# Four row-tiled products in a visit, one ring of five PSUM banks, three products per tile into one accumulator bank

## The chip, the cores and the metric

The kernel runs on one core of one Trainium2 chip. The metric is the device time in microseconds (us) of one launch, from three runs. The engines are named as in the profile: PE (TensorE matmuls), PEld (its weight loads), DVE (VectorE), ACT (ScalarE), POOL (GpSimd), SP (SyncE, which issues most DMAs).

## The reference, cut to what matters

The reference is a layer of a perceiver: cross-attention of 512 latent rows over 8192 context rows, then a Mamba-like block with an MLP, then a mixture of 16 experts with a shared expert. The change touches the cross-attention, and the tail through the PSUM banks that it hands on.

```python
x = x + xattn(layernorm(x), ctx, ctx, Wq, bq, Wk, bk, Wv, bv, Wo, bo)   # x 512x512, ctx 8192x512
x = x + attn(layernorm(x), ...)      # state-space block, MLP
x = x + ffn(layernorm(x), ...)       # 16 experts, top 2, shared expert

def xattn(Q, K, V, ...):             # 16 heads of 64
    q = (1 / 8) * (Q @ Wq + bq);  k = K @ Wk + bk;  v = V @ Wv + bv
    a = softmax(einsum('nlhd,nshd->nhls', q, k))
    o = einsum('nhls,nshd->nlhd', a, v)
    return o @ Wo + bo
```

## The kernel before

**Precision by splitting.** The kernel is held to float32 accuracy with float16 products. An operand is split into a high and a low float16 part, and a product is made of three: high x high, high x low, low x high.

**Passes.** The 16 heads are 8 pairs, and a pass (`filler`, L421) works for two pairs at a time, so there are 4 passes (`NPASS`). Each goes over the context in 16 chunks of 512 rows (`NCH`). For a chunk it makes the keys of both pairs (`kproj_units`, L246, two groups of 12 products of 512 columns), and the values (`vproj_units`, L266, two groups of 24 products of 256 columns), and stores them in DRAM (`k_d`, `v_d`). A value row of a head holds low part (64), a zero, high part (64) and a constant 16: `VW` = 130.

**Maximum pass.** Softmax needs each row's maximum before the exponentials. `smax_units` (L286) makes a rough score of the chunk for it, from the high parts alone. The contraction is 64 long, so the two heads of a pair stand in the upper and the lower 64 rows of PE, and their two products (L297, 512 columns) can run side by side. ACT copies each bank to `sf` (L302), and DVE takes the running maximum (L310) once four copies are there. One turn of this is called a visit here. In the first pass (`wide`) a visit has four products, in two pairs, with banks of `ps_x` and `ps_s`; in passes 2 to 4 it has two, with the two banks of `ps_x`, and `yield 406` after each.

**Attention.** A unit is a pair of heads and half of the 512 rows (16 units), and has 32 steps of 256 context rows (`NSTEP`). `scores` (L345) makes 8 products of 256 columns (L359, L360) into two banks of `ps_s`, 2 to a bank and head; ACT takes the exponential to float32 (L367, two instructions). In even steps ACT takes it a second time to float16 for the high part (L369); in odd steps DVE casts it (L371). DVE subtracts for the low part (L372). `av` (L375) multiplies with the values: 8 products of 130 columns with the high part as weights (L389), which give high x low and high x (high, row sum) side by side, and 8 of 65 columns with the low part (L392). They pile up over the 32 steps in `po0` and `po1`, a bank for each head. `unit_end` (L394) adds the halves, divides by the row sum, turns the result (L410, a bank of `bank_j`) and splits it.

**PSUM.** There are 8 banks: `ps_s` 2, `ps_o` 2 (`po0`, `po1`), `ps_x` 2, `ps_j` 2. `bank_j` (L126) hands out banks for projections and turns; outside of the attention it also uses `po1`. The tail's accumulators (`acc`, L647) use `ps_s`, `po0` and `ps_x`.

**Order.** The order of PE is written by hand up to the last unit (`manual_schedule`); the order of the other engines, and of PE after that, is a scheduler's. The filler is a generator that yields the planned PE time of each piece: 648 ns for 3 products of 512 or 6 of 256 columns, 406 for a visit of two. After every second piece (fourth in the first pass) `pump` gives one visit. The first pass runs alone. Passes 2 to 4 are woven into the first 380 steps (`NFILL`, L560): a step is scores, then pieces worth half of `rate`, then the `av` of an earlier step, then pieces worth the other half (L575 to L591). `rate` is the planned time of three passes (`PASSN`) over 380. The steps after that have no filler, and take the banks of `ps_x` for the scores of odd steps. The 16th unit is woven with the start of the tail (`tail`, L630), which does the rest of the layer. `weight_prep` (L509) brings in and splits the tail's weights on DVE in the first 380 steps, block by block as they land.

Of the kernel before, what the change touches and what calls it, by code (L numbers as in the profile page):

```python
# [16 lines left out]
P = 128  # L17
# [11 lines left out]
VW = 130  # L29
# [4 lines left out]
PASSN = 16 * (4 * 2592 + 8 * 406) + 2 * 2592 + 600  # L34
# [3 lines left out]
def perceiver_layer(ctx: ExitStack, tc: tile.TileContext, a: dict, out: bass.AP):  # L38
# [83 lines left out]
    ps_x = ctx.enter_context(tc.tile_pool(name="ps_x", bufs=2, space=PSUM))  # L122
    ps_j = ctx.enter_context(tc.tile_pool(name="ps_j", bufs=2, space=PSUM))
    jn = [0, True]

    def bank_j(shape, dtype, name):  # L126

        if jn[1]:
            jn[0] += 1
            if jn[0] % 3 == 0:  # L130
                return ps_o.tile(shape, dtype, name=name, tag="po1")
        return ps_j.tile(shape, dtype, name=name, tag="pj")
# [22 lines left out]
    for t in vss:  # L155
        nc.gpsimd.memset(t[:, :, :, 64:65], 0.0)
        nc.gpsimd.memset(t[:, :, :, 129:130], WS)
# [108 lines left out]
    def vproj_units(g, c, ct, w, j):  # L266
# [13 lines left out]
        nc.scalar.copy(vs[:, :, :, 65:129], pv)  # L280
        nc.vector.tensor_tensor(vs[:, :, :, 0:64], pv, vs[:, :, :, 65:129], ALU.subtract)  # L281
# [4 lines left out]
    def smax_units(c, qh, kh, runm, wide):  # L286

        for q2 in range(2):
            sf = sb3.tile([P, 2, 2, CH], F16, name="sf", bufs=2)
            pss = []  # L290
            for qi in range(2):
                qt = 2 * q2 + qi
                for hh in range(2):
                    s = slice(hh * 64, hh * 64 + 64)
                    pool, tag = (ps_s, "pss") if wide and qi else (ps_x, "px")
                    ps = pool.tile([P, CH], F32, name="psx", tag=tag)
                    nc.tensor.matmul(ps, lhsT=qh[s, qt * P : (qt + 1) * P], rhs=kh[s, 0, :], start=True, stop=True)  # L297
                    pss.append((sf[:, qi, hh, :], ps))
                if wide and not qi:
                    continue  # L300
                for dst, ps in pss:
                    nc.scalar.activation(dst, ps, AF.Copy, scale=1.0 / (8.0 * WS))  # L302
                pss = []
                if not qi:
                    yield 406
# [5 lines left out]
            yield 626 if wide else 406  # L311
# [33 lines left out]
    def scores(u, m, ld, sp, alone=False):  # L345
# [6 lines left out]
        for i in range(2):  # L352
            t = (m % 4) * 2 + i
            sl = slice(t * P, (t + 1) * P)
            pool, tag = (ps_x, "px") if alone and m % 2 else (ps_s, "pss")
            ps = pool.tile([P, 2, HQ], F32, name="pss", tag=tag)
# [18 lines left out]
    def av(po, m, x):  # L375
# [3 lines left out]
        for x in range(2):  # L379
            for i in range(2):  # L380
                t = (m % 4) * 2 + i
                for hh in range(2):
                    vv = v[:, t, hh]
                    for qt in range(2):
                        o, qs = po[hh][:, qt, :], slice(qt * P, (qt + 1) * P)
                        first = m == 0 and i == 0 and qt == 0
                        last = m == NSTEP - 1 and i == 1
                        if x == 0:
                            nc.tensor.matmul(o, lhsT=ph[:, i, hh, qs], rhs=vv, start=first, stop=False, **kw)  # L389
                        else:  # L390
                            o, vv_ = o[:, 65:VW], vv[:, 65:VW]
                            nc.tensor.matmul(o, lhsT=pl[:, i, hh, qs], rhs=vv_, start=False, stop=last, **kw)  # L392

    def unit_end(u, po, sp):  # L394
# [26 lines left out]
    def filler():  # L421
# [23 lines left out]
        for g in range(NPASS):  # L445
# [14 lines left out]
            for c in range(NCH):  # L460
# [93 lines left out]
    jn[1] = False  # L554
# [10 lines left out]
    def drain():  # L565
        pu, pm, px = pend.pop(0)
        if pm == 0:
            po[:] = [ps_o.tile([P, 2, VW], F32, name=f"po{hh}", tag=f"po{hh}") for hh in range(2)]
        av(po, pm, px)
        if pm == NSTEP - 1:  # L570
            e = unit_end(pu, po, sp[0])
# [33 lines left out]
    for m in range(NSTEP):  # L605
# [7 lines left out]
        if m == 0:  # L613
            tl = tail(tc, a, out, const, scr, ident, x_sb, mlp_d, oT, y_d, xd_d, (ps_s, ps_o, ps_x, bank_j))
# [7 lines left out]
    jn[1] = True  # L622
# [7 lines left out]
def tail(tc, a, out, const, scr, ident, x_sb, mlp_d, oT, y_d, xd_d, psums):  # L630
# [5 lines left out]
    ps_s, ps_o, ps_x, bank_j = psums  # L636
# [722 lines left out]
```

## Time and profile before

| what | us |
|---|---|
| median of 3 runs (lowest, highest) | 2652.26 (2648.97, 2652.97) |
| profiled execution | 2653.45 |
| its span, first to last instruction | 2651.7 |
| first pass alone | 0 to 278.5 |
| steps 1 to 380, with passes 2 to 4 | 278.5 to 1644.6 |
| steps 381 to 480 | 1644.6 to 1809.8 |
| last unit, with the start of the tail | 1809.8 to 1914.5 |
| tail | 1914.5 to 2651.7 |

The stretches are cut at the starts of the score products. The granted PE clock over the span is 0.959 of full speed.

The costliest groups that the change touches; columns: line, engine, operation, out<-in, shape, count, busy us, mean ns of one, idle time of the engine before them and who ended it:

```profile
L302 ACT ACTIVATE sf<-psx 128x512 f16<-128x512 f32 x1024 | 557.7, 622 | 79.1 <-PE psx L297 77.2
L389 PE MATMUL po<-v,phl 128*128 128x130 f16 x4096 | 327.2, 222 | 5.2 <-DVE oq L402 4.7
L297 PE MATMUL psx<-khl,qh 64*128 64x512 f16 x1024 | 212.5, 395 | 21.3 <-ACT sf L302 18.4
L392 PE MATMUL po<-v,phl 128*128 128x65 f16 x4096 | 209.9, 194 | 9.3 <-DVE phl L372 9.3
```

The mean length of a matmul is the time from its start to its end, and matmuls overlap: a product of 65 columns is 194 ns long, while eight of them follow each other within 0.24 us. So what a product costs PE is read from the distance of two starts, in the view that lists instructions in order of time. The busy time of a group counts overlapping instructions once.

### The profile page before, as it was taken

To read this page: it belongs to the slowest core of one execution; us is meant where nothing else is said; L and a number is where in the kernel's file an instruction comes from. 1 tells how busy PE (TensorE), PEld (TensorE's weight loads), DVE (VectorE), ACT (ScalarE), POOL (GpSimd) and SP (SyncE) were. 2 spreads that over 40 slices of the span, in tenths; PEclk is the share of its full clock that TensorE was granted. 3 is DMA by queue.
4 is the path that set the end of the run, shared out by engine and by line. 5 is a ranking of instruction groups with operands and counts; after the bars stand their busy time and mean duration, and the time that the engine had idled before them with its cause. 6 is when DMAs were issued, how large, how long until landed. Compare 5 with 4: busy or idle time off the path is not lost. (4 is left out here: it accounts for less than half of the span.)

```text
span 2651.7 us, 54346 instructions
## 1 busy us (share of the span) xinstructions
PE 2410.6 (91%) x21806; PEld 1693.5 (64%) x21806; DVE 2049.4 (77%) x2403; ACT 1955.5 (74%) x3734; POOL 44.2 (2%) x58
## 2 busy tenths in 40 slices
PE   7999998999999899998999998998878688998895
PEld 4454676777666677766677766997656466665442
DVE  6876688877877877777877777997899999633785
ACT  5787787888787788867788887997868476432784
POOL 2000000000000000000000000000000000001001
PEclk9999999999899999989999998999989889999998
DMA  7973899866598866658966655887511322675896
GB/s 265 308 255 128 268 284 270 242 169 187 166 268 264 265 189 176 184 152 250 253 176 190 173 162 129 201 204 206 171 56 41 96 72 82 229 233 200 294 337 222
DMA packets 353686, 531.42 MB, mean 200 GB/s; under 512 B 25106, under 2 KB 218834, under 8 KB 353300
## 3 DMA queue, kind: packets, MB, share of 16 engines
q1 hardware_dynamic: 352148, 523.69, 65.6%
q0 software_dynamic: 1280, 4.20, 0.5%
q8 instruction: 173, 2.83, 0.5%
q14 instruction: 85, 0.70, 0.1%
HBM read 397.68 MB, written 126.94 MB: 198 GB/s over the span
## 5 line engine op out<-in xcount | busy, mean ns | idle before, releaser
L372 DVE TENSOR_TENSOR phl<-p,phl 128x1024 f16<-128x1024 f32 x512 | 625.9, 1224 | 175.0 <-ACT phl L369 158.9
L367 ACT ACTIVATE p<-pss 128x512 f32<-128x512 f32 x1024 | 596.8, 619 | 126.1 <-PE pss L360 50.7
L302 ACT ACTIVATE sf<-psx 128x512 f16<-128x512 f32 x1024 | 557.7, 622 | 79.1 <-PE psx L297 77.2
L359 PE MATMUL pss<-qhh,k 128*128 128x256 f16 x2048 | 486.2, 277 | 18.5 <-ACT phl L369 18.0
L360 PE MATMUL pss<-qlm,kb 128*128 128x256 f16 x2048 | 485.2, 276 | 0.6 <-DMA kb<-k_d 0.4
L389 PE MATMUL po<-v,phl 128*128 128x130 f16 x4096 | 327.2, 222 | 5.2 <-DVE oq L402 4.7
L310 DVE TENSOR_TENSOR runm<-runm,sf 128x2048 f16<-128x2048 f16 x240 | 292.4, 1218 | 45.7 <-ACT sf L302 45.2
L389 PEld LDWEIGHTS <-phl 128*128 128x128 f16 x4096 | 273.9, 99 | 69.4 <-issue 21.5
L369 ACT ACTIVATE phl<-pss 128x512 f16<-128x512 f32 x512 | 312.3, 610 | 0.0
L274 PE MATMUL psv<-wh_v,ctxc 128*128 128x256 f16 x1024 | 283.4, 277 | 7.7 <-DVE khl L258 3.4
L275 PE MATMUL psv<-wl_v,ctxc 128*128 128x256 f16 x1024 | 282.2, 276 | 1.2 <-DVE wl_v L176 1.2
L276 PE MATMUL psv<-wh_v,ctxc 128*128 128x256 f16 x1024 | 282.1, 276 | 0.0
L359 PEld LDWEIGHTS <-k 128*128 128x128 f16 x2048 | 202.2, 99 | 63.7 <-issue 18.0
L360 PEld LDWEIGHTS <-kb 128*128 128x128 f16 x2048 | 202.7, 99 | 61.0 <-issue 22.2
L297 PE MATMUL psx<-khl,qh 64*128 64x512 f16 x1024 | 212.5, 395 | 21.3 <-ACT sf L302 18.4
L371 DVE CAST phl<-p 128x1024 f16<-128x1024 f32 x256 | 176.1, 688 | 58.1 <-ACT p L367 57.7
L392 PE MATMUL po<-v,phl 128*128 128x65 f16 x4096 | 209.9, 194 | 9.3 <-DVE phl L372 9.3
L250 PE MATMUL psk<-ctxc,wh_k 128*128 128x512 f16 x512 | 198.6, 388 | 21.1 <-DVE vs L281 10.5
L919 PE MATMUL py<-hs,ident 128*128 128x256 f32 x512 | 148.1, 447 | 67.1 <-DVE hs L916 67.0
L251 PE MATMUL psk<-ctxc,wh_k 128*128 128x512 f16 x512 | 197.2, 385 | 0.7 <-DVE ctxc L234 0.7
L252 PE MATMUL psk<-ctxc,wl_k 128*128 128x512 f16 x512 | 196.8, 384 | 0.0
L392 PEld LDWEIGHTS <-phl 128*128 128x128 f16 x4096 | 172.8, 98 | 12.8 <-DVE phl L372 12.0
(304 smaller groups left out, 3711.9 us busy)
## 6 DMA issues: line engine op xcount, KB each, us to landing
v<-v_d SPq DMA_DIRECT2D x128, 520.0 KB, 4.4
k<-k_d SPq DMA_DIRECT2D x256, 256.0 KB, 5.8
ctxc<-ctx_d SPq DMA_DIRECT2D x96, 512.0 KB, 5.2
wef<-in_gu_dram SPq DMA_DIRECT2D x72, 512.0 KB, 5.9
v_d<-vs SPq DMA_DIRECT2D x128, 260.0 KB, 3.8
k_d<-khl SPq DMA_DIRECT2D x128, 256.0 KB, 4.2
kb<-k_d SPq DMA_DIRECT2D x128, 256.0 KB, 5.4
wpm<-w_d SPq DMA_DIRECT2D x48, 512.0 KB, 3.9
```

The costliest lines, as they stand in the source:

```text
L274: nc.tensor.matmul(ps[:, t, :], lhsT=ct[i // 2][:, 0, i % 2, sl], rhs=wh[:, i, :], start=i == 0, stop=False)
L275: nc.tensor.matmul(ps[:, t, :], lhsT=ct[i // 2][:, 0, i % 2, sl], rhs=wl[:, i, :], start=False, stop=False)
L276: nc.tensor.matmul(ps[:, t, :], lhsT=ct[i // 2][:, 1, i % 2, sl], rhs=wh[:, i, :], start=False, stop=i == NC4 - 1)
L302: nc.scalar.activation(dst, ps, AF.Copy, scale=1.0 / (8.0 * WS))
L310: nc.vector.tensor_tensor(r, r, sf, ALU.max)
L359: nc.tensor.matmul(ps[:, hh], lhsT=k[:, hh, sl], rhs=qhh[:, hh, qs], start=True, stop=False)
L360: nc.tensor.matmul(ps[:, hh], lhsT=b[:, hh, sl], rhs=qlm[:, hh, qs], start=False, stop=True)
L367: nc.scalar.activation(p32[:, i], pss[i], AF.Exp, scale=sc)
L369: nc.scalar.activation(ph[:, i], pss[i], AF.Exp, scale=sc)
L372: nc.vector.tensor_tensor(pl, p32, ph, ALU.subtract)
L389: nc.tensor.matmul(o, lhsT=ph[:, i, hh, qs], rhs=vv, start=first, stop=False, **kw)
L392: nc.tensor.matmul(o, lhsT=pl[:, i, hh, qs], rhs=vv_, start=False, stop=last, **kw)
```

## The change

Four edits that belong together:

- `bank_j` hands out one ring of five banks, `ps_j`, for projections, turns, the products of the maximum pass, the scores of odd steps where there is no filler, and the tail. `ps_x` is gone, and so is the switch `jn`.
- A visit of the maximum pass has four products in every pass, two after two. It yields 640, and `pump` gives one after every fourth piece: in the middle of each group of pieces in passes 2 to 4, at its end in the first.
- A value row loses its zero (`VW` = 129, low 64, high 64, constant). `av` multiplies high x (high, row sum), 65 columns, and then high x low, 64 columns, into the same 64 columns, and low x (high, row sum) as before: 24 products in a step, with a weight load each, where there were 16.
- Both heads of a unit pile up in one bank, `po`. `unit_end` has no halves to add: one reciprocal, and a product for each head that reads PSUM.

```diff
-VW = 130
+VW = 129
...
-PASSN = 16 * (4 * 2592 + 8 * 406) + 2 * 2592 + 600
+SMAXN = 640
+PASSN = 16 * (4 * 2592 + 4 * SMAXN) + 2 * 2592 + 600
...
-    ps_x = ctx.enter_context(tc.tile_pool(name="ps_x", bufs=2, space=PSUM))
-    ps_j = ctx.enter_context(tc.tile_pool(name="ps_j", bufs=2, space=PSUM))
-    jn = [0, True]
+    ps_j = ctx.enter_context(tc.tile_pool(name="ps_j", bufs=5, space=PSUM))
 
     def bank_j(shape, dtype, name):
-        if jn[1]:
-            jn[0] += 1
-            if jn[0] % 3 == 0:
-                return ps_o.tile(shape, dtype, name=name, tag="po1")
         return ps_j.tile(shape, dtype, name=name, tag="pj")
...
-        nc.gpsimd.memset(t[:, :, :, 64:65], 0.0)
-        nc.gpsimd.memset(t[:, :, :, 129:130], WS)
+        nc.gpsimd.memset(t[:, :, :, 128:129], WS)
...
-        nc.scalar.copy(vs[:, :, :, 65:129], pv)
-        nc.vector.tensor_tensor(vs[:, :, :, 0:64], pv, vs[:, :, :, 65:129], ALU.subtract)
+        nc.scalar.copy(vs[:, :, :, 64:128], pv)
+        nc.vector.tensor_tensor(vs[:, :, :, 0:64], pv, vs[:, :, :, 64:128], ALU.subtract)
...
-                    pool, tag = (ps_s, "pss") if wide and qi else (ps_x, "px")
-                    ps = pool.tile([P, CH], F32, name="psx", tag=tag)
+                    ps = ps_s.tile([P, CH], F32, name="psx", tag="pss") if wide and qi else bank_j([P, CH], F32, "psx")
                     nc.tensor.matmul(ps, lhsT=qh[s, qt * P : (qt + 1) * P], rhs=kh[s, 0, :], start=True, stop=True)
                     pss.append((sf[:, qi, hh, :], ps))
-                if wide and not qi:
-                    continue
-                for dst, ps in pss:
-                    nc.scalar.activation(dst, ps, AF.Copy, scale=1.0 / (8.0 * WS))
-                pss = []
-                if not qi:
-                    yield 406
+            for dst, ps in pss:
+                nc.scalar.activation(dst, ps, AF.Copy, scale=1.0 / (8.0 * WS))
...
-            yield 626 if wide else 406
+            yield SMAXN
...
-            pool, tag = (ps_x, "px") if alone and m % 2 else (ps_s, "pss")
-            ps = pool.tile([P, 2, HQ], F32, name="pss", tag=tag)
+            if alone and m % 2:
+                ps = bank_j([P, 2, HQ], F32, "pss")
+            else:
+                ps = ps_s.tile([P, 2, HQ], F32, name="pss", tag="pss")
...
-                    vv = v[:, t, hh]
+                    vl, vh1 = v[:, t, hh, 0:64], v[:, t, hh, 64:129]
                     for qt in range(2):
-                        o, qs = po[hh][:, qt, :], slice(qt * P, (qt + 1) * P)
-                        first = m == 0 and i == 0 and qt == 0
+                        o, qs = po[:, hh, qt, :], slice(qt * P, (qt + 1) * P)
+                        first = m == 0 and i == 0 and hh == 0 and qt == 0
                         last = m == NSTEP - 1 and i == 1
                         if x == 0:
-                            nc.tensor.matmul(o, lhsT=ph[:, i, hh, qs], rhs=vv, start=first, stop=False, **kw)
+                            nc.tensor.matmul(o, lhsT=ph[:, i, hh, qs], rhs=vh1, start=first, stop=False, **kw)
+                            nc.tensor.matmul(o[:, 0:64], lhsT=ph[:, i, hh, qs], rhs=vl, start=False, stop=False, **kw)
                         else:
-                            o, vv_ = o[:, 65:VW], vv[:, 65:VW]
-                            nc.tensor.matmul(o, lhsT=pl[:, i, hh, qs], rhs=vv_, start=False, stop=last, **kw)
+                            nc.tensor.matmul(o, lhsT=pl[:, i, hh, qs], rhs=vh1, start=False, stop=last, **kw)
...
-        for hh in range(2):
-            nc.scalar.copy(oq[:, :, hh, :], po[hh][:, :, 0:64])
-        for hh in range(2):
-            nc.vector.reciprocal(rl[:, hh], po[hh][:, :, VW - 1])
-            nc.vector.tensor_tensor(oq[:, :, hh, :], po[hh][:, :, 65:129], oq[:, :, hh, :], ALU.add)
+        nc.vector.reciprocal(rl, po[:, :, :, 64])
         for hh in range(2):
             nc.vector.tensor_tensor(
-                oq[:, :, hh, :], oq[:, :, hh, :], rl[:, hh].unsqueeze(2).to_broadcast((P, 2, 64)), ALU.mult
+                oq[:, :, hh, :], po[:, hh, :, 0:64], rl[:, hh].unsqueeze(2).to_broadcast((P, 2, 64)), ALU.mult
             )
...
-                        if k % (2 if g else 4) == 0:
+                        if k % 4 == (2 if g else 0):
                             yield from pump()
...
-            po[:] = [ps_o.tile([P, 2, VW], F32, name=f"po{hh}", tag=f"po{hh}") for hh in range(2)]
-        av(po, pm, px)
+            po[:] = [ps_o.tile([P, 2, 2, 65], F32, name="po", tag="po")]
+        av(po[0], pm, px)
...
         if nacc[0] % 3 == 0:
-            return ps_o.tile([P, DM], F32, name="acc3", tag="po0")
-        return ps_x.tile([P, DM], F32, name="acc4", tag="px")
+            return ps_o.tile([P, DM], F32, name="acc3", tag="po")
+        return bank_j([P, DM], F32, "acc4")
```

In the changed kernel the lines that matter are L243 to L245 (keys), L267 to L269 (values), L289 (maximum pass) and L292 (its copies), L348 and L349 (scores), L356 and L358 (exponentials), L378, L379 and L381 (values' products), L395 (turn at a unit's end).

More of the change, by code (lines that the diff above doesn't have):

```diff
@@ L553, in perceiver_layer @@
         advance(done[0] + 1)
-    jn[1] = False
     start = done[0]
@@ L567, in drain @@
         if pm == 0:
-            po[:] = [ps_o.tile([P, 2, VW], F32, name=f"po{hh}", tag=f"po{hh}") for hh in range(2)]
-        av(po, pm, px)
+            po[:] = [ps_o.tile([P, 2, 2, 65], F32, name="po", tag="po")]
+        av(po[0], pm, px)
         if pm == NSTEP - 1:
-            e = unit_end(pu, po, sp[0])
+            e = unit_end(pu, po[0], sp[0])
             next(e)
@@ L613, in perceiver_layer @@
         if m == 0:
-            tl = tail(tc, a, out, const, scr, ident, x_sb, mlp_d, oT, y_d, xd_d, (ps_s, ps_o, ps_x, bank_j))
+            tl = tail(tc, a, out, const, scr, ident, x_sb, mlp_d, oT, y_d, xd_d, (ps_s, ps_o, bank_j))
         for _ in range(2):
@@ L621, in perceiver_layer @@
         pass
-    jn[1] = True
     while not ready:
@@ L635, in tail @@
     U32 = mybir.dt.uint32
-    ps_s, ps_o, ps_x, bank_j = psums
+    ps_s, ps_o, bank_j = psums
     nacc = [0]
```

## The prediction

> **What bounds the kernel now.** I read the span and busy shares first, then the busy time by stage, then single instructions in order of time, then PE's waits.
>
> The stages, cut at the score steps (columns: stretch, length, busy us and count for PE, PEld, DVE, ACT, POOL, granted clock, DMA share, GB/s):
>
> ```profile
> span 2651.7 us, 54346 instructions
> PE 2410.6 (91%) x21806; PEld 1693.5 (64%) x21806; DVE 2049.4 (77%) x2403; ACT 1955.5 (74%) x3734; POOL 44.2 (2%) x58
> 0.00:278.50 278.50, 254.71 (x1550) 135.34 (x1551) 197.44 (x231) 199.21 (x366) 19.50 (x25) 0.95 0.71 238
> 278.50:1644.60 1366.10, 1306.71 (x13314) 939.20 (x13313) 1054.56 (x1261) 1098.92 (x2148) 2.29 (x6) 0.97 0.73 211
> 1644.60:1809.80 165.20, 161.13 (x2437) 150.03 (x2434) 157.28 (x174) 154.06 (x310) 0.00 (x0) 1.00 0.82 204
> 1914.50:2651.70 737.20, 600.80 (x3534) 397.60 (x3534) 560.08 (x608) 419.46 (x748) 21.61 (x24) 0.93 0.49 168
> ```
>
> The second stretch holds the 380 steps in which passes 2 to 4 are woven into attention. PE is 96% busy there, ACT 80%, DVE 77%. A busy PE need not be a full one, so I looked at starts. Here is half a step, and a visit of the first pass, which already has four products:
>
> ```profile
> 1004.51 0.27 PE L359 MATMUL pss<-qhh,k 128*128 128x256 f16 x1
> 1004.62 0.27 PE L360 MATMUL pss<-qlm,kb 128*128 128x256 f16 x1
> 1004.82 0.39 PE L297 MATMUL psx<-khl,qh 64*128 64x512 f16 x2
> 1005.15 0.63 PE L389 MATMUL po<-v,phl 128*128 128x130 f16 x8
> 1005.62 0.41 PE L392 MATMUL po<-v,phl 128*128 128x65 f16 x8
> 1005.86 0.27 PE L274 MATMUL psv<-wh_v,ctxc 128*128 128x256 f16 x1
> ...
> 202.26 0.38 PE L251 MATMUL psk<-ctxc,wh_k 128*128 128x512 f16 x1
> 202.48 0.38 PE L252 MATMUL psk<-ctxc,wl_k 128*128 128x512 f16 x1
> 202.79 0.60 PE L297 MATMUL psx<-khl,qh 64*128 64x512 f16 x4
> 203.33 0.28 PE L274 MATMUL psv<-wh_v,ctxc 128*128 128x256 f16 x1
> ...
> 203.48 2.05 ACT L302 ACTIVATE sf<-psx 128x512 f16<-128x512 f32 x4
> ```
>
> The reader is to see starts, not lengths: products of 256 columns start 0.109 us apart, of 512 columns 0.216, of 130 columns 0.059 (0.47/8), of 65 columns 0.030 (0.24/8), each with its own weight load. Adding up the median distances of every kind of neighbours in 290 to 1600 us gives 1215 of 1310 us: PE streams at its own pace, and 95 us are waits. A steady step takes 3.31 us. What PE is spared here, the kernel is spared. In the 100 steps after the passes a step takes 1.576 us, which is again the sum of PE's starts (8 x 0.109, 0.46, 0.24). The tail is another matter: its scans are on DVE.
>
> PE's waits in the second stretch (us, times, longest):
>
> ```profile
> PE psx L297 <- ACT sf L302: 12.4, 15, 2.1
> PE psk L250 <- DVE vs L281: 10.5, 2, 6.7
> PE pto L410 <- DVE vs L281: 10.2, 3, 6.5
> PE po L392 <- DVE phl L372: 7.5, 8, 1.8
> PE pss L359 <- ACT phl L369: 7.3, 11, 3.9
> ```
>
> **The change, part by part.** Sums are made on the profiled execution, 2653.45 us (span 2651.7 and 1.75 around it), which is 1.2 over the median of 2652.26.
>
> *Visits of four.* Entering the row-tiled products costs a gap: 0.20 us from L360 to L297 where 0.109 is usual, 0.31 where 0.216 is usual, so 0.096 both times. Then 0.322 us pass from the first of a pair to the next ordinary product, 0.537 for four. A visit of two costs 0.418, of four 0.634; two become one, so 0.202 us are saved. There are 3 passes x 16 chunks x 4 = 192: **-38.8 us**. In 343 of 379 visits the pair starts together; in the others it is paced by ACT, which the change doesn't quicken, so the low end is 0.905 of it, -35. After a visit the next product but one is 10 ns late, which gives the high end, -40.7.
>
> *Three products per tile.* A step had 8 products of 130 columns and 8 of 65; it gets 16 of 65 and 8 of 64. The build has 4096 more weight loads and as many more matmuls. Median starts add to 462 + 240 ns now; three runs of eight at 240 make 720: 18 ns x 512 steps = **+9 us**, all of it on PE. No row shows a 64-column product into the columns that the one before it just wrote. The bounds come from the row of 65 columns: most start 29 ns apart (24 x 29 = 696, -3 us), two in each eight 34 (if all did: 816, +58 us). The router's products of 16 columns, which do pile up in one place with a load each, start 25 ns apart; so I stay with 30.
>
> A page speaks against this part. The Trainium skill, "TensorE: Matmul & The Clock Gate", section Back-to-back issue gap, gives a stream of load and matmul pairs about 81 ns each at 128 columns; by it 4096 more pairs would be an estimated +332 us and the kernel near 2985. The row of 130 columns, 59 ns apart, disagrees with the page.
>
> *ACT gets four copies at once.* ACT's order follows PE's in both builds. Now a visit of two that stands right before the scores delays the first exponential from 0.69 to 1.07 us after the scores start, and in even steps (four exponentials) the slack of the second score bank falls from 0.99 to 0.60 (medians of 89 and 41 steps). With four copies of 0.488 each, started about 0.13 before the scores, the first exponential comes at 1.82, so 1.13 late: slack -0.14, less 0.04 for the shorter step, and spread by the unevenness of the steps (some 0.26). That is 0.22 us on average. The built order has 36 such visits: **+8 us**; from 0 to 0.5 each, so 0 to +18. Odd steps have 2.0 us of slack. What waits behind is PE's next score product, and with it all of PE.
>
> *One ring of five.* A projection had two banks and two L250 waits and three L410 waits on a late DVE (20.7 us, with L274 24.1). DVE was late because it stood behind weight blocks that had not landed. In the build, projections take a bank that ACT emptied (in passes 2 to 4 none waits for its own predecessor), and the fourth product of a visit takes the old projection's, half a group later. PE can run further before it must wait, but ACT and the score banks stop it next. I take less than half: **-10**, between 0 and -24. At the ends of the passes four visits stand in a row and ACT sets the pace with two banks or five: **0**, by the 12.4 us of L297's row plus or minus 5.
>
> *One accumulator bank.* The end of a unit loses two copies on ACT (0.28 each) and one reciprocal; the next unit's first product waits for both heads' multiplications instead of for its own head's addition. L389 now waits 1.1 us at most, 4.7 in all. **-2**, between -5 and +4. The two heads share what is queued on DVE behind.
>
> *Elsewhere.* V rows shrink from 260 to 258 bytes a head; the queue's orders are as many as before. First pass: same four products. Tail: L1209 waits 5.7 us for a bank that a ring of five has to spare; the order of PE in the last unit moves. **-4**, between -10 and +8.
>
> Sum: -38.8 + 9 + 8 - 10 - 2 - 4 = -37.8, so 2615.6 in the terms of the profiled run, **2615** near the median.
>
> Another page warns of the third part: the Trainium skill, "TensorEngine Tiling (Array Packing)", section PSUM Bottleneck, says that row tiling quickens PE and not the copies out of PSUM. Here the copies of a visit take 2.05 us against 0.63 on PE; what that does is the 8 us above, since ACT has a fifth of the stage free.
>
> **Rivals.** *The bursts eat it.* If every even-step visit and half the odd ones met a late exponential, about 140 of the 192 at 0.22 us, 31 us would go instead of 8, and 2638 remain; if each of the 192 lost 0.2 us, the visits' whole gain would be gone: 2647 to 2658, no change (a measurement of this kernel tells 0.2%, 5 us, from none). For: 80% busy ACT and only two score banks. Against: one fill unit between visit and scores (0.65 us) already restores the slack.
>
> *Slower: the added products don't stream.* One mechanism, at L378 and L379: a product that adds to the columns just written, with the same weights loaded again, holds the next back. It decides from 30 ns + 37.8 us/4096 = 39 ns a product. At the 59 ns of the 130-column row it costs 4096 x 30 ns = 123 us more than forecast: 2738; at 45 ns, 2676. For: no row has this pattern at this width. Against: 16 columns at 25 ns, 65 at 30.
>
> *The ring doesn't do what it says.* If banks went round strictly, each projection would wait for its predecessor's copy and subtraction (0.70 + 0.75 us and the passing on, less 0.7 of attention between): 0.9 x 192 = 170 us, 2786. The build's waits speak against it: first products of a projection wait for ACT, those of a visit's fourth for DVE.
>
> **How the numbers follow.** Forecast, with bursts up to the 2638 above, 0.75; bursts that eat all of the gain 0.10 (0.07 of it no change, 0.03 slower), products that don't stream 0.11, the ring 0.04. Faster 0.75, same 0.07, slower 0.18. Adding the parts' bounds as independent errors (2, 8, 8, 8, 5, 4, 7) gives 17, and 1.28 times that either way makes the forecast's own range 2593 to 2637. Since 0.18 lies far above it, the range that is to hold 8 in 10 reaches a little lower, to 2590, and over most of the bursts' case, to 2652.
>
> **What would show it.** Visits at L289 in fours, 0.54 us from first to next; L378 with L379 60 ns a pair; the steady step at 3.31 - 0.10 + 0.02 = 3.23 us; after the passes 1.59; L348 waiting for exponentials some 15 us in place of 7; L243 and L395 waiting less than 21. A pair at L378/L379 near 90 ns, or L348 waiting over 40 us, proves me wrong.

## The result, and the profile after

The changed kernel takes 2661.16 us (median of 20 runs, 2647.49 to 2668.62), the kernel before 2648.48 us beside it (20 runs, 2643.11 to 2658.57). The ratio is 1.0041, interval 1.0028 to 1.0054: slower by 11 us (the medians lie 12.7 us apart), where 38 less were forecast; it also lies above the forecast's range, 2590 to 2652. The profiled execution took 2657.44 us, only 4.0 more than the one of before, so the stages below show 4 of the 11 us. From its page, span and PE:

```profile
span 2655.7 us, 62337 instructions
PE 2386.4 (90%) x25902; PEld 1697.9 (64%) x25902; DVE 2048.5 (77%) x2355; ACT 1943.1 (73%) x3704; POOL 41.4 (2%) x55
```

PE is busy for 24 us less although it has 4096 more matmuls. So PE's own work did become shorter, and it stands longer. Busy time by stage, cut as before, the last unit included, which ends with its last `av` product (columns as before: stretch, length, PE, PEld, DVE, ACT, POOL, clock, DMA share, GB/s):

```profile
0.00:275.50 275.50, 249.76 (x1549) 134.06 (x1550) 200.25 (x231) 199.20 (x366) 19.22 (x22) 0.95 0.71 238
275.50:1625.20 1349.70, 1282.27 (x16336) 941.26 (x16335) 1050.94 (x1228) 1084.18 (x2126) 2.29 (x6) 0.98 0.73 213
1625.20:1792.80 167.60, 163.59 (x3254) 153.23 (x3251) 156.08 (x165) 153.50 (x304) 0.00 (x0) 1.00 0.81 201
1792.80:1911.50 118.70, 94.09 (x1242) 73.81 (x1238) 80.11 (x128) 87.62 (x165) 0.74 (x3) 0.88 0.60 173
1911.50:2655.70 744.20, 596.66 (x3535) 395.51 (x3534) 561.12 (x605) 418.62 (x745) 19.16 (x24) 0.93 0.48 166
```

Against the stages of before: the first pass -3.0, steps 1 to 380 -16.4 (some -35 was forecast), steps 381 to 480 +2.4 (+1.8 was forecast), the last unit +14 (104.7 before), the tail +7.

What the edits do on PE is what was forecast for them. A half step of the changed kernel, from the instructions in order of time:

```profile
1000.45 0.27 PE L349 MATMUL pss<-qlm,kb 128*128 128x256 f16 x1
1000.66 0.61 PE L289 MATMUL psx<-khl,qh 64*128 64x512 f16 x4
1001.20 0.20 PE L378 MATMUL po<-v,phl 128*128 128x65 f16 x1
1001.24 0.20 PE L379 MATMUL po<-v,phl 128*128 128x64 f16 x1
1001.27 0.19 PE L378 MATMUL po<-v,phl 128*128 128x65 f16 x1
```

The visit lasts 0.54 us to the next product, and L378 and L379 follow each other by 30 ns. Now the waits of PE in steps 1 to 380 (us, times, longest):

```profile
PE psx L289 <- DVE khl L251: 24.6, 15, 4.7
PE psx L289 <- DVE vs L274: 13.2, 11, 3.3
PE pss L348 <- ACT phl L358: 8.8, 22, 0.6
...
PE psx L289 <- ACT sf L292: 3.1, 4, 1.4
```

The projections' waits of before on a late DVE are gone, and the products of the maximum pass have them instead: khl and vs are subtractions in a projection's bank. Measured by starts, as what the four products of a visit take beyond the clean 3, 223 and 3 ns, PE loses 64.4 us inside the visits (11.0 before), 55.7 of it ahead of the fourth product. The longest case, on DVE and on PE:

```profile
798.66 0.76 DVE L520 TENSOR_SCALAR mph<-mpf 128x512 f16<-128x512 f32 x2 [3.85 <-DMA mpf<-in_w_dram]
799.34 1.28 DVE L521 SCALAR_TENSOR_TENSOR mph<-mpf,mph 128x512 f16<-128x512 f32 x2
800.54 1.22 DVE L361 TENSOR_TENSOR phl<-p,phl 128x1024 f16<-128x1024 f32 x1
801.68 1.22 DVE L297 TENSOR_TENSOR runm<-runm,sf 128x2048 f16<-128x2048 f16 x1
802.82 0.69 DVE L360 CAST phl<-p 128x1024 f16<-128x1024 f32 x1
803.54 1.22 DVE L361 TENSOR_TENSOR phl<-p,phl 128x1024 f16<-128x1024 f32 x1
804.68 0.74 DVE L251 SCALAR_TENSOR_TENSOR khl<-psk,bk_sb,khl 128x512 f16<-128x512 f32 x1
```

```profile
800.22 0.60 PE L289 MATMUL psx<-khl,qh 64*128 64x512 f16 x3
805.48 0.58 PE L289 MATMUL psx<-khl,qh 64*128 64x512 f16 x1 [4.66 <-DVE khl L251]
```

DVE stands 3.85 us before a weight block that has not landed. Behind it in DVE's order stand four instructions of the split, the exponentials' subtractions, and at last L251, which frees a bank at 805.4. Three products of the visit had their banks; the fourth gets this one and starts at 805.48, and PE, in order too, has done nothing for 4.7 us.

Not every late case is of this kind. In the trace of the changed kernel 42 fourth products wait for DVE, 51.5 us in all. For 47 us of it, instructions of the weights' split stand on DVE in the 6 us before. A wait of DVE for a block that had not landed stands there for 28 us of it, or for 40 us if one looks 8 us back. The rest comes behind the work of the split alone, some 0.9 us for each pair of instructions. Below, "late DVE" means both, and no run takes them apart.

For the experiments, steps 1 to 380 are cut in two: the waits are what the starts of PE's instructions lie beyond the median distance of the same pair of neighbours, where the trace names a releaser; the rest is PE's own pace.

| kernel | steps 1 to 380 | own pace | waits |
|---|---|---|---|
| before | 1366.1 | 1294.9 | 71.3 |
| changed | 1349.7 | 1258.2 | 91.6 |

The pace fell by 37 us and the waits rose by 20. By the product that waits, before and after, in us: products of the maximum pass 30 and 69 (with the waits between visits that stand in a row), projections and turns 21 and 6, `av` 11 and 2, scores 11 and 15. The forecast comes to some -32 us of pace and -2 of waits here, so what it missed in this stretch is in the waits.

### The profile page after: what moved, and what is told of

The parts are those of the page before. It is cut to its first block, busy times and chain, and to the rows that moved or that the text cites. A ratio compares the mean times of both kernels' runs of the same rounds, so it can differ in the third digit from the quotient of the medians.

```text
span 2655.7 us, 62337 instructions
## 1 busy us (share of the span) xinstructions
PE 2386.4 (90%) x25902; PEld 1697.9 (64%) x25902; DVE 2048.5 (77%) x2355; ACT 1943.1 (73%) x3704; POOL 41.4 (2%) x55
## 5 line engine op out<-in xcount | busy, mean ns | idle before, releaser
L361 DVE TENSOR_TENSOR phl<-p,phl 128x1024 f16<-128x1024 f32 x512 | 625.5, 1224 | 137.9 <-ACT phl L358 123.3
L356 ACT ACTIVATE p<-pss 128x512 f32<-128x512 f32 x1024 | 604.6, 631 | 151.0 <-PE pss L349 75.3
L292 ACT ACTIVATE sf<-psx 128x512 f16<-128x512 f32 x1024 | 532.7, 628 | 84.7 <-PE psx L289 83.7
L348 PE MATMUL pss<-qhh,k 128*128 128x256 f16 x2048 | 485.8, 276 | 11.0 <-ACT phl L358 10.3
L349 PE MATMUL pss<-qlm,kb 128*128 128x256 f16 x2048 | 484.0, 275 | 0.1
L297 DVE TENSOR_TENSOR runm<-runm,sf 128x2048 f16<-128x2048 f16 x240 | 293.6, 1224 | 136.2 <-ACT sf L292 135.2
L378 PEld LDWEIGHTS <-phl 128*128 128x128 f16 x4096 | 286.8, 98 | 78.1 <-issue 50.3
L378 PE MATMUL po<-v,phl 128*128 128x65 f16 x4096 | 323.4, 195 | 6.3 <-DVE oq L389 3.6
L379 PE MATMUL po<-v,phl 128*128 128x64 f16 x4096 | 323.2, 194 | 0.0
L358 ACT ACTIVATE phl<-pss 128x512 f16<-128x512 f32 x512 | 316.9, 619 | 0.0
L267 PE MATMUL psv<-wh_v,ctxc 128*128 128x256 f16 x1024 | 284.5, 278 | 3.2 <-ACT wh_v L168 3.2
L379 PEld LDWEIGHTS <-phl 128*128 128x128 f16 x4096 | 273.1, 99 | 19.8 <-issue 0.3
L269 PE MATMUL psv<-wh_v,ctxc 128*128 128x256 f16 x1024 | 283.4, 277 | 0.0
L348 PEld LDWEIGHTS <-k 128*128 128x128 f16 x2048 | 202.2, 99 | 92.5 <-issue 37.3
L349 PEld LDWEIGHTS <-kb 128*128 128x128 f16 x2048 | 202.5, 99 | 55.9 <-issue 17.3
L289 PE MATMUL psx<-khl,qh 64*128 64x512 f16 x1024 | 184.3, 385 | 57.8 <-DVE khl L251 24.6
L381 PE MATMUL po<-v,phl 128*128 128x65 f16 x4096 | 209.7, 194 | 4.7 <-DVE phl L361 4.7
L243 PE MATMUL psk<-ctxc,wh_k 128*128 128x512 f16 x512 | 196.8, 384 | 8.5 <-ACT ctxc L226 8.5
```

The source lines that it names most:

```text
L267: nc.tensor.matmul(ps[:, t, :], lhsT=ct[i // 2][:, 0, i % 2, sl], rhs=wh[:, i, :], start=i == 0, stop=False)
L269: nc.tensor.matmul(ps[:, t, :], lhsT=ct[i // 2][:, 1, i % 2, sl], rhs=wh[:, i, :], start=False, stop=i == NC4 - 1)
L297: nc.vector.tensor_tensor(r, r, sf, ALU.max)
L348: nc.tensor.matmul(ps[:, hh], lhsT=k[:, hh, sl], rhs=qhh[:, hh, qs], start=True, stop=False)
L349: nc.tensor.matmul(ps[:, hh], lhsT=b[:, hh, sl], rhs=qlm[:, hh, qs], start=False, stop=True)
L356: nc.scalar.activation(p32[:, i], pss[i], AF.Exp, scale=sc)
```

## The experiments

Ratios are to the kernel before on the same chip, with 95% intervals; stages are of the one profiled execution, which can lie some us off the run's median (12 in e4).

**e1 and e2: the place of the visit.** The third or the first piece of a group in place of the second is followed by the visit (`k % 4 == (2 if g else 0)` in the change).

```diff
-                        if k % 4 == (2 if g else 0):
+                        if k % 4 == (3 if g else 0):     # e1
+                        if k % 4 == (1 if g else 0):     # e2
```

> The changed kernel with one thing moved: in passes 2 to 4 the visit of four comes after the third piece of a group and not after the second. Theory A (the fourth product takes the bank of the projection that ended half a group ago, and DVE has not emptied it; 64 us of waits at L289): one more piece (0.65 us) and on average most of a half step lie between, so the 43 long waits of 1.3 us on average shrink to some 20 us in all, steps 1 to 380 go from 1350 to about 1310 us, and the time is 2618 to 2635, ratio to before 0.988 to 0.995. Rival B (four copies in one go on ACT hold up the scores): the bursts stay, so the time stays, ratio 1.004. Rival C (the 24 products per step cost more than reckoned): no change either, 1.004. The last unit keeps its 119 us in all of them.

> The changed kernel with the visit after the first piece of a group. Theory A: DVE has one piece less to empty the old projection's bank, so far more of the 192 visits wait, 0.5 to 1 us more each: steps 1 to 380 grow by 60 to 130 us, ratio 1.03 to 1.05. Rivals B and C: as the changed kernel, 1.004.

Neither came as expected. e1: 1.0075 [1.0055, 1.0094], slower than the change and not faster; steps 1 to 380 1353.4 us, 57.1 us lost inside the visits, 24.0 of it by the fourth product on L251, in 11 cases and not 20. e2: 1.0226 [1.0201, 1.0251]; 1395.3 us, 120.7 lost, 108.4 of it by the fourth product: 50.3 on L251 in 43 cases, 25.8 on L274 in 36, 30.7 on ACT's copies in 38. One piece (0.65 us of PE) less between the old projection and the fourth product doubles the cases on both lines (on L274 they were 17). One more halves those on L251, but leaves 14 on L274, and the cases that are left are long: none of the three places covers a DVE that is 4 us late. That e2 loses time fits theory A and not its rivals; that e1 gains none does not fit it.

**e3: visits of two in the ring of five.** The change with the visits of before.

```diff
...
-            for dst, ps in pss:
+                if wide and not qi:
+                    continue
+                for dst, ps in pss:
...
+                if not qi:
+                    yield 406
...
-                        if k % 4 == (2 if g else 0):
+                        if k % (2 if g else 4) == 0:
```

> The changed kernel with the visits of two of the kernel before in passes 2 to 4 (after every second piece), in the ring of five. Theory A: the visits' gaps come back, 192 x 0.202 = +39 us, and the product that takes the old projection's bank comes a whole group later, so most of the 64 us of waits at L289 go: steps 1 to 380 about 1325 to 1340 us, ratio 0.996 to 1.002. Rival B: only the few us of scores' waits go, +39 remain, ratio 1.015 to 1.02. Rival C: +39, 1.018.

1.0032 [1.0019, 1.0046], as slow as the change, and slower than theory A had it. Steps 1 to 380 take 1348.9 us beside 1349.7: pace 1288.6 (30 more than with fours), waits 60.3 (31 less), 36.7 of them inside the visits. The fours' gain on PE is real and is lost in full to their waits. The last unit (118.3) and the tail (749.1) are long here too, so the visits are not what made them so.

**e4: three products and one accumulator alone.** The kernel before with the change's `av`, `unit_end` and value rows, and the banks `ps_x` 2 and `ps_j` 2 of before.

```diff
-VW = 130
+VW = 129
...
-            po[:] = [ps_o.tile([P, 2, VW], F32, name=f"po{hh}", tag=f"po{hh}") for hh in range(2)]
+            po[:] = [ps_o.tile([P, 2, 2, 65], F32, name="po", tag="po0")]
...
```

> The kernel before with the three products per tile and the one accumulator bank alone; the freed bank serves bank_j where po1 did (first pass and tail), and the main loop keeps ps_x 2 and ps_j 2. From the changed kernel's steps after the passes (1.607 us in place of 1.576) 31 ns x 512 steps = +16 us are to be expected: steps 381 to 480 168 us, steps 1 to 380 about 1376, ratio 1.004 to 1.008, and a last unit near the 105 us of before. Rival C, if the products explain what the forecast missed (48 us): ratio 1.015 or more.

1.0040 [1.0023, 1.0057], so +10.6 us of 2651.03 where the forecast had +9 - 2. A step behind the passes takes 1.607 us beside 1.576, +31 ns where 18 were forecast. The last unit stays at 104.2 us: three products are not what made it long.

**e5 and e6: the split of the weights on POOL**, in the changed kernel and in that of before.

```diff
-                nc.vector.tensor_scalar(hl[:, 0], f[:, sl], WF, None, ALU.mult)
-                nc.vector.scalar_tensor_tensor(hl[:, 1], f[:, sl], WF, hl[:, 0], ALU.mult, ALU.subtract)
+                nc.gpsimd.tensor_scalar(f[:, sl], f[:, sl], WF, None, ALU.mult)
+                nc.gpsimd.tensor_copy(hl[:, 0], f[:, sl])
+                nc.gpsimd.tensor_tensor(hl[:, 1], f[:, sl], hl[:, 0], ALU.subtract)
```

> The changed kernel with the splitting of the tail's weights moved from DVE to POOL (three instructions a half block: scale, cast, subtract). Theory D (DVE, in order, stands behind weight blocks that have not landed, and then behind their four instructions; the old projection's bank comes free that much later, and the ring of five hands it to the fourth product of a visit): without weight blocks on DVE the 64 us of waits at L289 in steps 1 to 380 fall below 25, the stretch goes from 1350 to 1300 to 1315 us, ratio to before 0.985 to 0.993. Theory A as first put (half a group is too short for DVE on any day): the waits stay above 45 us and the ratio above 1.0. POOL's own work may slow DVE where both go to SBUF; then the subtraction at L361 shows more than its 1.22 us.

> The kernel before with the same move to POOL. Theory D: it loses the waits of L250, L410 and L274 on a late DVE (24 us) and little else: steps 1 to 380 from 1366 to 1335 to 1345 us, ratio 0.988 to 0.994, so that the change is worth more than nothing with it: the one before this in the list should then be 15 to 40 us shorter in steps 1 to 380. Theory A: the 24 us go here too, but the changed kernel stays behind.

1.0107 [1.0087, 1.0128] and 1.0042 [1.0026, 1.0057]: both slower than their partners, steps 1 to 380 1367.9 and 1367.5 us; both expectations fell. The losses inside the visits fell in e5 to 47.1 us, some 16 of them in one case, so the waits that were meant to go did go in part; but the cure brought its own price. Score products now wait for their keys, in e5:

```profile
PE pss L348 <- DMA k<-k_d: 13.6, 7, 4.7
PE pss L349 <- DMA kb<-k_d: 10.3, 10, 2.3
```

That is 24 us, and 23 in e6; the kernels without POOL's split show less than 1 us of it. Why the keys come late was not tried. And POOL beside DVE slows DVE:

```profile
L361 DVE TENSOR_TENSOR phl<-p,phl 128x1024 f16<-128x1024 f32 x512 | 663.0, 1297 | 174.8 <-ACT phl L358 159.2 <-DMA xpf<-in_xp_dram 1.5 <-PE psx L289 0.9
```

That is e5's costliest group (line, engine, shape, count, busy us, mean ns, idle before); the mean is 1297 ns beside 1224 in the changed kernel. The 76 that took over 1.3 us all ran beside the split on POOL; of the 391 that did not, none took more than 1.23. A cure with side effects can't weigh the cause; e9 and e10 do it without POOL.

**e7 and e8: PE's order in the last unit by hand**, a piece of the tail in each step (e8 with e5's split as well).

```diff
+    ml = ExitStack()
+    ml.enter_context(tc.manual_schedule(engines=PE))
...
     for m in range(NSTEP):
-        for _ in range(2):
+        for _ in range(1):
```

> The changed kernel with PE's order written by hand in the last unit too, one piece of the tail after each step in place of the scheduler's order. Theory E (with a ring of five the scheduler puts the turn of the tail's first rows right behind the output projection, and PE stands 9.1 us for the layer norm on DVE and 4 us for a weight block): no such wait, the last unit goes from 119 to 100 to 106 us, everything else as in the changed kernel, ratio to before 0.998 to 1.001. Rival F (tail and scores contend for the five banks): the last unit stays near 119 us.

> The changed kernel with both: weights on POOL and the last unit by hand. If D and E hold, both gains add: steps 1 to 380 at 1300 to 1315 us, last unit at 100 to 106, ratio to before 0.980 to 0.988. If D falls, about the ratio of the last unit by hand alone.

1.0083 [1.0055, 1.0112] and 1.0167 [1.0142, 1.0192]. Both expectations fell. The last unit got longer, 135.3 and 134.4 us: in e7 the output projection now stood 8.8 us before weights that had not landed, the layer norm's turns 8.5 us before DVE. e12 tries the pieces further apart.

**e9 and e10: no split at all.** The blocks are fetched and stored as before, but without work on DVE; the tail's weights are zeros.

```diff
-                nc.vector.tensor_scalar(hl[:, 0], f[:, sl], WF, None, ALU.mult)
-                nc.vector.scalar_tensor_tensor(hl[:, 1], f[:, sl], WF, hl[:, 0], ALU.mult, ALU.subtract)
-                nc.sync.dma_start(dst[:, :, sl], hl)
+                nc.sync.dma_start(dst[:, :, sl], zz)      # zz: zeros
```

> The changed kernel without the 94 pairs of VectorE instructions that split the tail's weights into two halves between steps 0 and 380: the weight blocks are fetched and stored as before, but what is stored is zeros, so the tail works with weights of zero and only the stretch of steps 1 to 380 is to be read. Theory 'late DVE' (the fourth product of a visit inherits an old projection's bank and stands behind VectorE, which stands in order behind weight blocks that have not landed): the waits inside the visits fall from 64 us to under 25, the waits of the projections stay near nothing, and the stretch falls from 1349.7 us to 1290 to 1315 us. Rival 'ScalarE sets the visits': its copies of the same four banks stay as they are, the waits stay over 50 us, and the stretch stays above 1340 us. Rival 'PE's own pace': the stretch falls by less than 15 us although the waits go.

> The kernel before with the same cut (weights of zero in the tail, the fetches and stores kept); again only steps 1 to 380 are to be read. It shows what the cover of VectorE costs the old scheme of banks. Theory 'late DVE': the visits wait for ScalarE alone as before (11 us), only the 24 us of the projections' waits on late VectorE go, so the stretch falls from 1366 us to 1340 to 1350 us, and the changed kernel, freed of the same instructions, is ahead of it by 30 us or more, near the 35 us that were forecast. If both fall alike (the changed one ahead by 16 us as now), late VectorE is not what took the gain.

Steps 1 to 380 of the changed kernel (e9) and of that of before (e10), from busy time by stage:

```profile
297.10:1586.30 1289.20, 1260.29 (x16337) 933.04 (x16336) 963.97 (x1026) 1080.27 (x2126) 2.29 (x6) 0.99 0.70 207
```

```profile
294.60:1611.70 1317.10, 1289.03 (x13315) 931.52 (x13314) 969.16 (x1059) 1098.33 (x2148) 2.29 (x6) 0.99 0.69 202
```

and e9's waits of PE between 290 and 1600 us on khl and vs:

```profile
PE psx L289 <- DVE vs L274: 1.1, 3, 0.7
...
PE psx L289 <- DVE khl L251: 0.3, 1, 0.3
```

The loss inside the visits falls from 64.4 to 17.0 us, and the stretch by 60 us. The old scheme gains 49, more than expected, part of it at the cost of the first pass, which takes 22 and 16 us longer here because the weights' DMAs now run ahead in it (DMA share .87 and .89 there beside .71). The changed kernel leads by 28 us in the stretch, 16 with the split, so just short of the 30 that the theory asked for; its waits, 44.3, are now as few as the other's 42.6. The ratios turn round: 0.9878 [0.9859, 0.9897] and 0.9910 [0.9890, 0.9930]. The edit takes away two things at once, the waits for blocks and the split's own work on DVE (87 us of busy time in this stretch), and which of them weighs more stays open.

**e15: visits of two without the split**, the partner of e9 (e3 with e9's edit; the tail's weights are zeros).

> Visits of two in the ring of five, without the VectorE split of the tail's weights (weights of zero in the tail; only steps 1 to 380 are to be read): the partner of the changed kernel without the split, whose steps 1 to 380 took 1289.3 us. Theory 'visits of four are worth what was forecast, and late VectorE took it': with the split both took 1349 us; without it the fours lead by 20 to 38 us, so that this stretch is 1310 to 1327 us here. Rival 'visits of four are worth nothing in this kernel': 1284 to 1295 us.

```profile
290.90:1600.90 1310.00, 1290.28 (x16339) 941.43 (x16338) 964.15 (x1026) 1091.02 (x2126) 2.29 (x6) 0.99 0.70 204
```

With DVE on time the fours lead by 20.7 us (1289.3 and 1310.0), and by 21 us of the ratios (0.9878 and 0.9957 [0.9938, 0.9977]); with the split they tied. Pace 1245.0 and 1285.7: 41 us for the fours. Waits 44.3 and 24.3: 20 against them, 8.8 of it inside the visits and 7 at the scores behind ACT's four copies, the burst that had been forecast at 8.

**e11: rings of their own.** One accumulator and three products, but the freed bank goes to the projections, and visits come in twos from two banks of their own.

```diff
-    ps_j = ctx.enter_context(tc.tile_pool(name="ps_j", bufs=5, space=PSUM))
+    ps_x = ctx.enter_context(tc.tile_pool(name="ps_x", bufs=2, space=PSUM))
+    ps_j = ctx.enter_context(tc.tile_pool(name="ps_j", bufs=3, space=PSUM))
...
```

> One accumulator bank and three products per tile as in the change, but the freed bank goes to the projections alone (a ring of three) and the visits keep two banks of their own and come in twos, as before. Theory 'late DVE through the shared ring': no product of a visit can wait for VectorE; the visits' waits are near the 11 us of before (37 us with twos in the shared ring), the projections' waits on VectorE are under half of the 24 us of before, and steps 1 to 380 take 1335 to 1353 us beside 1349 with twos in the ring and 1377 with two banks for the projections. The order of PE in the last unit has the scores between the pieces of the tail again, so the last unit is near 104 us instead of 118. Time against before 0.994 to 1.000. Rival 'three products and one accumulator cost what was lost, and the ring nothing': 1.003 to 1.005, steps 1 to 380 near 1375 us.

0.9976 [0.9963, 0.9989], faster than before. Steps 1 to 380 take 1360.5 us, more than expected, with 11.4 us lost inside the visits but 22.4 behind late phl (L366 and L367) in front of the `av` products, a late DVE that is met at another place. The last unit and the tail, though, are short:

```profile
1803.80:1906.20 102.40, 88.41 (x1242) 71.93 (x1238) 79.61 (x128) 81.91 (x161) 0.74 (x3) 0.95 0.69 201
1906.20:2638.00 731.80, 599.35 (x3535) 398.72 (x3534) 559.89 (x605) 418.17 (x746) 21.30 (x24) 0.93 0.48 169
```

102.4 and 731.8 us, where e3, which differs in nothing but the shared ring, has 118.3 and 749.1.

**e12: the last unit by hand, spread out.** As e7, but the pieces go to steps 4, 5, 10 to 19, 21 and 22.

```diff
-        for _ in range(1):
+        for _ in range(m in (4, 5, 10, 11, 12, 13, 14, 15, 16, 17, 18, 19, 21, 22)):
...
```

> The changed kernel with PE's order in the last unit written out by hand: a step of scores and of products goes between any two pieces of the tail, the output projection of the first 15 units is begun at step 4 and the transposes of the layer norm wait until step 10, where the ring made the scheduler put them right behind the projection. Theory 'order': the last unit falls from 118.7 us to 100 to 107 us, the 9 us in which PE stood before the transposes and the clock of 0.75 behind them go, and the time against before falls from 1.004 to 0.998 to 1.001. Rival 'three products or the ring itself make the last unit slow': it stays above 113 us.

1.0098 [1.0071, 1.0125]; the last unit takes 127.4 us. The expectation fell. PE's waits in it:

```profile
PE pwo L692 <- DMA wpm<-Wo_d: 7.7, 2, 5.4
PE pt L669 <- DVE h L764: 5.5, 1, 5.5
PE po L378 <- DVE phl L360: 5.0, 3, 2.7
PE pss L348 <- ACT phl L358: 4.8, 5, 2.0
```

A piece written out in one block stands before whatever is late for it, and the scores behind it stand too. The scheduler's orders of e11 and of before break the pieces up (12 and 36 products of the projection with scores between them). Whether that, or the steps I chose, is the point was not tried.

**e13 and e14: the ring of five up to step 480, rings of their own behind it.** e13 is the changed kernel, e14 has visits of two (e3).

```diff
     attn.close()
     ms.close()
+    js.close()                      # gives the ring of five back
+    ps_x = [ctx.enter_context(tc.tile_pool(name="ps_x", bufs=2, space=PSUM)), "px"]
+    ps_j[0] = ctx.enter_context(tc.tile_pool(name="ps_k", bufs=3, space=PSUM))
...
```

> The changed kernel as it is up to step 480; there the ring of five is given back and two banks for the scores and three for the tail are opened in its place, so that only the last unit and the tail have rings of their own. Theory 'the shared ring spoils what comes after step 480 through the order that the scheduler then chooses': steps 1 to 380 stay at 1350 us, within 10, and step 381 to 480 at 167.5; the last unit falls from 118.7 to 101 to 106 us and the tail from 744.2 to 730 to 740 us, as with rings of their own throughout; against before 0.993 to 0.999 where the changed kernel had 1.0041. Rival 'one accumulator and three products lengthen the last unit and the tail': last unit and tail stay within 4 us, ratio 1.002 to 1.006. Rival 'what is won at the end is lost elsewhere': last unit at 101 to 106, but a ratio above 1.000.

> The same with visits of two in the ring of five (as in the run with visits of two), so that the two runs differ in the size of the visit alone, with an undisturbed end. If visits of four bring PE's pace and cost waits of the same size, the two agree within 0.2% and steps 1 to 380 within 10 us (1349 us both as before); if the visits of four are the better part of the change, this run is over 0.3% slower than the other; if they are the worse part, faster. Against before 0.993 to 0.998.

e13: 0.9939 [0.9915, 0.9963], 2632.27 us. e14: 0.9918 [0.9894, 0.9941], 2628.79 us. Both beat the kernel before. Steps 1 to 380 take 1352.7 and 1351.6 us, as in the changed kernel (1349.7); what went lies behind step 480. e13's last unit and tail:

```profile
1794.90:1897.30 102.40, 88.00 (x1241) 71.32 (x1237) 79.39 (x129) 81.74 (x161) 0.74 (x3) 0.97 0.72 201
1897.30:2630.90 733.60, 601.25 (x3534) 398.60 (x3534) 560.20 (x605) 419.19 (x746) 21.52 (x24) 0.93 0.48 168
```

What the order did, in the instructions of PE in order of time. The changed kernel, end of the output projection and the layer norm's turns:

```profile
1819.29 0.38 PE L691 MATMUL pwo<-wpm,oT 128*128 128x512 f16 x1
1828.72 2.00 PE L666 MATMUL pt<-ident,h 128*128 128x128 f32 x8 [9.05 <-DVE h L761]
1830.64 0.37 PE L683 MATMUL pxz<-hT,wpm 128*128 128x256 f16 x1
```

e13, the same two places:

```profile
1819.72 0.38 PE L697 MATMUL pwo<-wpm,oT 128*128 128x512 f16 x1
...
1824.37 0.60 PE L351 MATMUL pss<-qhh,k 128*128 128x256 f16 x4 [0.86 <-DMA k<-k_d]
1826.48 0.62 PE L384 MATMUL po<-v,phl 128*128 128x65 f16 x8 [1.51 <-DVE phl L364]
...
1831.52 0.44 PE L672 MATMUL pt<-ident,h 128*128 128x128 f32 x2
```

With the shared ring the scheduler puts the turns right behind the projection, and PE stands 9 us, with the attention's work behind them, until the layer norm is done. With rings apart it puts scores and `av` products between, and the turns wait for nothing. The changed kernel's last unit also has a wait of 4.0 us for a weight block (L689; 1.3 in e13); the two make up most of the 16 us that e13 is shorter there. That the ring is the cause is shown by e13. The last unit takes 115 to 119 us in every run that shares the ring to the end and leaves the order to the scheduler (e1, e2, e3, e5, e9 and e15 as well), and 102 to 106 in those that do not share it (before, e4, e6, e10, e11, e13, e14). The tail is less clear: 742 to 749 us against 732 to 739, but 744.6 in e4, which does not share the ring and whose execution lay 12 us over its median. That the ring acts through the order is read from the trace: e7 and e12, with an order by hand, did not bring the gain.

## Why the prediction was wrong, point by point

The runs make a chain from before to the changed kernel (ratio differences times 2650 us):

| step | forecast | measured |
|---|---|---|
| three products, one accumulator, ring of five, own rings at the end (before to e14) | -3 | -22 (0.9918) |
| visits of four in place of two (e14 to e13) | -31 | +6, its interval includes 0 |
| the shared ring behind step 480 (e13 to the change) | -4 | +27 |
| sum | -38 | +11 |

By the intervals of the ratios the three measured steps are good to about 6, 9 and 7 us either way.

- *Visits of four, -38.8.* As a price on PE it was right: 0.538 us a visit, and the pace parts by 41 us between e15 and e9. That the kernel is spared what PE is spared was wrong. Without the weights' split half of it arrives (20.7 of 41 us), and with the split nothing (e3, e13 and e14).
- *One ring of five*, and here the forecast's failing step: "the fourth product of a visit takes the old projection's, half a group later. PE can run further before it must wait". The bank was read right and the wait was not priced. Half a group is 1.3 us of PE; DVE was up to 5 us late, behind weight blocks and their split. The same lateness that cost the projections 24 us costs 53 us more than before inside the visits (39 more, 30 to 69, when the waits between visits in a row are counted too). I took the relief of the old waits (-10) and no price for the new one. As a ring for visits of two it was better than forecast: e4 to e14 is -32 us; steps 1 to 380 are 25 us shorter, of 41 between the two profiled executions.
- *Elsewhere*, the second failing step: "the order of PE in the last unit moves", -4 between -10 and +8. I saw that the order moves and didn't ask what PE would stand before in the new one. The shared ring costs 27 us in last unit and tail (16 and 11 by stages). In the tail's scans DVE waits 10.2 us for ACT in front of `lgu` and `ex` in the changed kernel and 3.8 in e13. That comes with the ring; through which instruction was not tried.
- *Three products per tile, +9, and one accumulator, -2*: +10.6 for both together (e4). Right, a little short: 31 ns a step and not 18 behind the passes. The rival of products that don't stream is out, with 30 ns between L378 and L379.
- *ACT's bursts, +8*: L348 waits 8.8 us on phl and not 15. Counted by starts, fours make the scores wait for ACT 5 us more than twos (e3 to the change, and e14 to e13), and 7 us more without the split (e15 to e9). Right in sign and a little under the forecast.
- *The rivals.* The strict ring came nearest: a bank that must be waited for. I gave it 0.04 and priced it for the projections, at 170 us, and it came at the visits, at 53. The 0.18 for a slower kernel was given for other mechanisms than the one that came, and neither of the two signs that were to prove the forecast wrong was seen: L378 with L379 take 60 ns a pair, and L348 waits 8.8 us.

## What to carry to other kernels

When rings of buffers are merged, ask for each taker whose buffer it inherits, and price that releaser's lateness and not its distance: the slowest queue behind any bank of the ring becomes a wait of all that use it. An order that a scheduler chooses is part of such a change: read what it puts behind a long chain of small instructions, here a layer norm. Keep the ring where it pays, and give it back where it doesn't (e14: 20 us under the kernel before).

## What the runs showed of the hardware

PE's granted clock falls when it has stood, and stays low for some us behind: in the changed kernel's last unit, where PE stands 9.05 us up to 1828.72, it is 0.74 between 1819 and 1831 us, with PE busy for 2.9 of 12 us, and behind it the products of 256 columns start 0.213 us apart up to 1835.0 and 0.109 after that. So a wait is paid for twice. Shorter waits did it too: in e12 PE is busy for 1.3 of the 6.0 us up to 1872.6, with no wait over 3 us; then the clock is 0.60 between 1873 and 1888, and the distance is again 0.213. POOL's element-wise work beside DVE's lengthens DVE's L361: from 1224 to 1297 ns on average over the whole of e5, and there only where the two ran side by side. Products of 64 and 65 columns that add to the columns the one before has just written, each with a weight load of its own, start 29 to 30 ns apart.
